# Splitting the row checks, row sums on ScalarE, and a new end for the first stream: an fp32 gated graph network followed by a graph convolution

## The chip, the cores and the metric

One core of one Trainium2 chip. The metric is the device time of the kernel in microseconds (us), the median of three runs. The core's engines are TensorE (PE, with its weight loads PEld), VectorE (DVE), ScalarE (ACT), GpSimd (POOL) and SyncE (SP, which here only issues DMAs).

## The reference

16 graphs of N = 1024 nodes with C = 128 features, fp32. `adj` holds 0 and 1 and is symmetric by its construction. The node mask is all ones.

```python
def _gru_cell(m, h, w_ih, w_hh, b_ih, b_hh):
    ...
    r = sigmoid(xr + hr); z = sigmoid(xz + hz)
    n = tanh(xn + r * hn)
    return (1.0 - z) * n + z * h

def _L0_gnn_ref(x, adj, mask, weight, w_ih, w_hh, b_ih, b_hh):
    h = x
    for i in range(4):
        hw = einsum('bnc,cd->bnd', h, weight[i])
        m = einsum('bjn,bjd->bnd', adj, hw)
        h = _gru_cell(m, h, w_ih[i], w_hh[i], b_ih[i], b_hh[i])
    return h * mask[:, :, None]

def _L1_gnn_ref(x, adj, W, b, gamma, beta):
    h = x
    for i in range(4):
        h = einsum('bnm,bmc->bnc', adj, h @ W[i]) + b[i]
        h = relu(h)
        mu, var = mean(h, axis=(0, 1)), variance(h, axis=(0, 1))
        h = gamma[i] * (h - mu) * rsqrt(var + EPS) + beta[i]
    return h

x = x + _L0_gnn_ref(relu(layernorm(x)), adj, nodemask, ...)
x = x + _L1_gnn_ref(relu(layernorm(x)), adj, ...)
```

## The kernel before

A first phase, here the gate phase, computes the gated layers, a second one, conv, the convolution layers, and a third one writes the output. Features lie on the partitions and nodes along the row (128x1024), cut in two halves of 512 nodes[...].

**The gate phase** has two streams: `sa` takes the graphs 0, 2, ..., 14 and `sb` the graphs 1, 3, ..., 15. `half_step(one, two)` (L1095) lets PE aggregate for stream `one` (32 matmuls `pm <- row, ghw` at L524, adjacency rows against a split of hW into a high and a low fp32r part) while stream `two` passes its gates: 12 fp32 products at L993, each 128x512 and recorded as two matmuls, for r, n and z of both halves. The two change places after each half-step, so a cycle of four layers has eight half-steps, and there are 64 in all. `clock[0]` counts half-steps. Every engine's order in this phase is the order in which the program calls (`manual_schedule`), and work that isn't part of a half-step is put on an agenda: `at(n, place, fn)` enters it for half-step n, and `due(place)` runs it at a named place.

In a half-step, stream `two` does for each half: the products; `reset_gate` (ACT L1011, sigmoid of r); `candidate` (DVE L1012 r*hn, L1013 + xn, then ACT L1016 tanh); `less` (DVE L1029); `update_gate` (ACT L1020, sigmoid of z; DVE L1033); `mixed` (DVE L1034, the new h). ACT's `high` (L919 or L938) and DVE's `low` (L926 or L942) make the split of hW of stream `one`. At its end `agg_rows` copies `pm` to `m` on ACT (L955); the next half-step's products start with `g_r <- h` and go on with `g_r <- m`. The PSUM banks are reused: the second half's `g_hn` needs the bank that L1012 of the first half reads, and the second half's `g_z` the bank that L1020 reads.

**The next graph's rows.** While a stream is in its last layer (i = 3), `fetch` (L853) asks SP for rows 0 to 3 of the adjacency of the graph after next in this stream, into a staging area of four slots; POOL casts them to fp32r (`round_rows`, L577); `last_four` (L866) then checks them, and asks for rows 4 to 7 in the same slots. The check reads the low 16 bits of each value and tells whether the rounding was exact: on ACT it is a `glance` (L586, an activation with a sum, two instructions in the trace), on DVE a `look` (L610, a maximum). For `sa` (its i = 3 half-step is called A here) rows 4 to 7 are looked at by DVE at "start" of the next half-step (B); in B the staging serves `sb`, whose rows 4 to 7 are glanced at on ACT at "gap" of the half-step after (C).

The transposed adjacency goes to DRAM for conv (`adjT_d`, POOL casts at L615, SP transposes, POOL stores, `mids` at L1088). h is not transposed by PE between layers: `half_out` writes a DVE transpose of 32x32 blocks, `exchange_out` and `exchange_in` (or `pair_in`) bring it back by DMA with the blocks in place. Only the last h of the graphs 14 and 15 is turned by PE, in `tail_sums` (L735, `pt_x`), since `last_tail` (L757) calls it without exchanged parts; its inner `rest` normalizes (L668 to L680, `rs_mid`, `ms_mid`, `y_mid`) and stores y for conv.

**Conv.** For each layer and graph b, `load_adjT` brings eight rows of the transposed adjacency in bf16 (`block`, `packed`), and ACT and DVE widen them to fp32r (L1311, L1313), into the same slots that the rows of the gate phase use. `aggregate` does 32 matmuls of L524. In layer 0 PE takes the adjacency before the weights: `first_split` (L1366) loads y and splits it (chw, ACT L1370, DVE L1371); after b's aggregation, `first_weights` copies it out of PSUM (cm, ACT L1380) and multiplies with the weights (`pw`, L1381), two for each graph; this is called half an aggregation later. Here PE, POOL and SP follow the program's calls around the end of the gate phase, and the remaining order on ACT and DVE is made by the framework's scheduler. `row_sums` (L1402) has PE sum the rows of graph 0's adjacency into all partitions (`pt_deg`, L1407), which ACT copies to `degree` (L1411); `raw_weights` uses it from layer 1 on.

Of the kernel before, what the change touches and what calls it, by code (L numbers as in the profile page):

```python
# [16 lines left out]
P = 128  # L17
# [324 lines left out]
def exact_path(  # L342
# [39 lines left out]
    def tmp(name):  # L382
        return ps_t.tile([P, HALF], F32, tag="tmp", name=name)

    adjT_d = [dram.tile([NB, P, N], BF16, tag=f"adjT{b}", name=f"adjT_d{b}") for b in range(B)]
    xmid_d = [dram.tile([N, C], F32, tag=f"xmid{b}", name=f"xmid_d{b}") for b in range(B)]
    ymid_d = [dram.tile([P, N], F32, tag=f"ymid{b}", name=f"ymid_d{b}") for b in range(B)]
# [20 lines left out]
    nc.vector.memset(eps_t, EPS)  # L408
    ones = const.tile([P, 1], F32, tag="ones", name="ones")
    nc.vector.memset(ones, 1.0)  # L410
    low = const.tile([P, (B + 2) * NB], F32, tag="low", name="low")
    nc.vector.memset(low, 0.0)

# [119 lines left out]
    with ExitStack() as st:  # L533
# [51 lines left out]
                k = b * NB + j  # L585
                nc.scalar.activation(junk, lows, AF.Copy, accum_out=low[:, k : k + 1])  # L586

        def exchange_out(t, name, d=None):
            if d is None:
                d = rawd.tile([P, HALF], F32, tag="cross", name=f"cross_{name}", bufs=8)  # L590
            nc.sync.dma_start(d, t)
            return d

        def exchange_in(d, t):
# [2 lines left out]
            for s in range(4):  # L597
                nc.sync.dma_start(t[s * 32 : (s + 1) * 32, :].rearrange("r (t x) -> r t x", t=4), src[s])

        def pair_in(d, t):  # L600

            src = d.rearrange("h (t r) (s x) -> s r (h t) x", t=4, s=4)
            for s in range(4):
                nc.sync.dma_start(t[s * 32 : (s + 1) * 32, :].rearrange("r (a x) -> r a x", a=8), src[s])

        def look(b, row, j, part=0):

# [108 lines left out]
                half_out(cross_tile(f"t_{name}_{hf}"), src, hf, name, d[hf])  # L716
            return d

        def half_out(t, src, hf, name, d=None):
            turned = nc.vector.transpose(by_nodes(t), four_ways(src[:, hf * HALF : (hf + 1) * HALF]))  # L720
            return exchange_out(t, f"{name}_{hf}", d), turned

        def cross_tile(name):
            return half_tile(name).bitcast(F32)
# [30 lines left out]
            nc.gpsimd.dma_start(ymid_d[b], y)  # L755

        def last_tail(b, xt, hT):  # L757
            nt = tail_sums(b, xt, hT)
            y = y_mid(b) if b + 1 < B else xt.rearrange("p k c -> p (k c)")
            store_xmid(b, xt)  # L760

            def rest():
                norm_apply(xt, y, nt)
                store_ymid(b, y)

            return rest
# [3 lines left out]
        class Stream:  # L770
# [54 lines left out]
            def plan(self, n, tail=None):  # L825

                if tail:
                    b, xt, hT, parts = tail
                    end = {}

                    def sums():
                        end["norm"] = tail_sums(b, xt, hT, parts)

                    def blocks(hf):
                        if hf == 0:
                            end["y"] = y_mid(b)
                        norm_blocks(xt, end["y"], end["norm"], range(hf * BH, (hf + 1) * BH))

                    at(n + 2, "gap", sums)
                    at(n + 3, "mid", lambda: store_xmid(b, xt))  # L840
                    at(n + 3, "gap", lambda: norm_factors(end["norm"]))
                    at(n + 4, "beside0", lambda: blocks(0))
                    at(n + 4, "beside1", lambda: blocks(1))
                    at(n + 5, "mid", lambda: store_ymid(b, end["y"]))
                if self.b + 2 < B:
                    at(n + 5, "mid", self.next_load)
                    at(n + 6, "start", self.next_sums)
                    at(n + 6, "gap", self.next_factors)
                    at(n + 7, "beside0", lambda: self.next_blocks(0))
                    at(n + 7, "beside1", lambda: self.next_blocks(1))  # L850
                    at(n + 7, "end", self.ins_away)

            def fetch(self):  # L853

                if self.i == 3 and self.b + 2 < B and not written[0]:
                    if self is sa:
                        t = turned_tile(f"stage{self.b + 2}").bitcast(F32)
                        room[0] = [t[:, 2 * q : 2 * q + 2, :].rearrange("p a n -> p (a n)") for q in range(4)]
                    self.stage = room[0]
                    stage_rows(self.b + 2, self.stage, range(4))  # L860

            def first_four(self):
                if self.stage:
# [2 lines left out]
            def last_four(self):  # L866
                if self.stage:
                    b, stage, self.stage = self.b + 2, self.stage, None
                    glance(b, stage, range(4))
                    stage_rows(b, stage, range(4, NB))  # L870
                    self.rows += round_rows(b, stage, range(4, NB))

                    def looks():
                        for j in range(4, NB):
                            look(b, stage[j % 4], j)

                    if self is sa:
                        at(clock[0] + 1, "start", looks)
                    else:
                        at(clock[0] + 1, "gap", lambda: glance(b, stage, range(4, NB)))  # L880

            def take(self):
                self.xt, self.y = self.next_x, self.next_y
# [6 lines left out]

            def half_away(self, hf):

                if self.i + 1 - hf == L and self.b + 2 < B:
                    if hf == 0:
                        self.pair = rawd.tile([NH, P, HALF], F32, tag="pair", name=f"pair_out{self.b}", bufs=4)
                    half_out(cross_tile(f"t_out{self.b}_{hf}"), self.new, hf, f"out{self.b}", self.pair[hf])
                elif self.turned_away(self.i + 1 - hf):
                    nm = f"{self.b}_{self.i + 1 - hf}"
                    out, self.last_dve = half_out(cross_tile(f"t_h{nm}_{hf}"), self.new, hf, f"h{nm}")
                    self.outs.append(out)  # L900
# [138 lines left out]
            def finish(self):  # L1039

                if self.i < L:
                    return
                args = self.b, self.xt, self.hT
                self.b, self.i = self.b + 2, 0
                if self.b >= B:
                    self.rest = last_tail(*args)
                    return
                self.take()
                ins, outs, h_in = self.next_ins, self.pair, self.hT
                parts = [args[-1][:, hf * HALF : (hf + 1) * HALF] for hf in range(NH)]  # L1050

                last = args[-1]
                at(clock[0] + 1, "ins", lambda: pair_in(ins, h_in))
                at(clock[0] + 1, "outs", lambda: pair_in(outs, last))
                self.plan(clock[0], (*args, parts))
# [3 lines left out]
        def at(n, place, go):  # L1059
            agenda.setdefault((n, place), []).append(go)  # L1060
# [5 lines left out]
        def first_step(one, two, gated, halfway):  # L1066
# [10 lines left out]
            feed.some(1)  # L1077
            two.gate_step(1)
            two.half_away(1)
            gated()  # L1080
            one.agg_step(0)
            halfway()
# [12 lines left out]
        def half_step(one, two, gated=None, halfway=None):  # L1095
# [18 lines left out]
            two.products(0)  # L1114
            two.reset_gate(0)
            due("beside0")
            two.candidate(0)
            two.less(0)
            one.high(0)
# [9 lines left out]
            two.products(1)  # L1129
            two.reset_gate(1)  # L1130
            due("beside1")
            one.low(1)
            two.candidate(1)
            two.less(1)
# [20 lines left out]
        with tc.manual_schedule(engines=every):  # L1155
# [115 lines left out]

            sa.plan(0)
            sb.plan(1)
            first_step(sa, sb, looks, lambda: ahead(1))
            first_step(sb, sa, lambda: turn_ih(prep, w_g, 2), lambda: ahead(2))
            written[0] = False
# [6 lines left out]
        with tc.manual_schedule(engines={getattr(mybir.EngineType, e) for e in ("PE", "Pool", "SP")}):  # L1283
            sb.gate_step(0)
            sb.gate_step(1)
            with tc.issue_after(sb.last_act.ins):
                sa.rest()
            sb.finish()


    worst = small.tile([P, 1], F32, tag="worst", name="worst")
# [74 lines left out]
    def first_split(b):  # L1366
        yt = flat(f"y{b}").rearrange("p k c -> p (k c)")
        nc.gpsimd.dma_start(yt, ymid_d[b])
        hw = hw_tiles(b, f"chw{b}_0")
        nc.scalar.copy(hw[0], yt)  # L1370
        nc.vector.tensor_sub(hw[1], yt, hw[0].bitcast(F32))  # L1371
        return hw

# [17 lines left out]
    def raw_weights(i, pm, aff, stats):  # L1391
# [6 lines left out]
            nc.vector.scalar_tensor_tensor(mt[:, cols], degree[:, cols], aff[1], mt[:, cols], ALU.mult, ALU.add)  # L1398
            nc.tensor.matmul(pc[hf], w_c[:, i, :], mt[:, cols], start=True, stop=True)
        conv_done(0, i, pc, stats)  # L1400

    def row_sums(rows):  # L1402

        pd = [tmp(f"pt_deg{hf}") for hf in range(NH)]
        for j in range(NB):
            for hf in range(NH):
                nc.tensor.matmul(  # L1407
                    pd[hf], ones_r, rows[j][:, hf * HALF : (hf + 1) * HALF], start=(j == 0), stop=(j == NB - 1)
                )
        for hf in range(NH):  # L1410
            nc.scalar.copy(degree[:, hf * HALF : (hf + 1) * HALF], pd[hf])  # L1411

    xo = []

# [29 lines left out]
            for n0, n in pieces(k):  # L1444
                nc.gpsimd.dma_start(xo_piece(k, n0, n), by_node(xmid_d[k], n0, n))

    ones_r = work.tile([P, P], F32R, tag="ones_r", name="ones_r", bufs=1)
    nc.vector.tensor_copy(ones_r, ones.to_broadcast([P, P]))
    degree = w_mT.rearrange("p l c -> p (l c)")[:, :N]

    stats = small.tile([P, B * NH, 6], F32, tag="bn_st", name="stats0")
# [1 line left out]
    for b in range(B):  # L1453
# [9 lines left out]
        if b == B - 1:  # L1463
            hw_next = raw_split(1)
        aggregate(pm, hw, rows, 1)
        if b == 0:
            row_sums(rows)
        hw, waiting = hw_next, (b, pm)


# [112 lines left out]
```

## Time and profile before

| | us |
|---|---|
| median of three runs | 1788.79 |
| fastest, slowest run | 1787.79, 1789.32 |
| the profiled execution | 1789.26 |
| its span | 1787.5 |
| one half-step of the gate phase | 17.57 |
| aggregation of graph 0 in conv begins at | 1166.99 |
| output phase, from | 1759.3 |

The profile belongs to one execution. Its timeline has one line for a group of neighbouring instructions: start, time from first start to last end, engine, line of the kernel, operation, output <- input, shape, count, and in brackets the idle time before it and what ended that. Ends of PE instructions are modelled, and the first matmul after an fp32 product is recorded some 0.4 us early, so intervals between starts are a better measure on PE than busy time. In the table of waits a line gives who waited, for whom, the sum in us, the number of waits and the longest.

### The profile page before, as it was taken

Reading aid. Unit: us, or ns where it says so; the run is one execution under the profiler, and the core shown is the slowest. Engines: PE = TensorE matmul, PEld = TensorE weight load, DVE = VectorE, ACT = ScalarE, POOL = GpSimd, SP = SyncE. Lnnn points to the kernel's source line nnn. Section 1 sums busy time; section 2 is a strip of 40 time slices with the busy share of each in tenths; the row PEclk is TensorE's granted clock in tenths of the full one; section 3 lists DMA queues with packets and bytes.
Section 4 is the critical chain, followed back from the end, with each engine's and each line's share of the span. In section 5 each row is a group of like instructions: output and inputs, shape, how many; then the busy total and the mean of one; then the engine's idle time right before and its main releaser. Section 6 shows DMA issues by size and latency. Waiting matters only on the chain. (4 is left out here: it accounts for less than half of the span.)

```text
span 1787.5 us, 22335 instructions
## 1 busy us (share of the span) xinstructions
PE 1759.3 (98%) x6734; PEld 1191.7 (67%) x6734; DVE 1305.9 (73%) x2310; ACT 1107.6 (62%) x1713; POOL 379.3 (21%) x417
## 2 busy tenths in 40 slices
PE   9999999999999999999999999999999999999997
PEld 6565655565656565556555556577778888888886
DVE  7677877887887787887797787676666666666665
ACT  5356556556566556665655655476777767768765
POOL 4314323332331331422432333010100000000011
PEclk9999999999999999999999999999999999999999
DMA  7467657777676676776756768788766575767667
GB/s 259 135 175 262 189 163 272 179 208 241 204 200 213 223 212 197 245 202 202 260 169 186 265 174 227 256 287 311 271 228 241 207 253 201 245 224 245 238 217 268
DMA packets 363617, 400.16 MB, mean 224 GB/s; under 512 B 158188, under 2 KB 239888, under 8 KB 363488
## 3 DMA queue, kind: packets, MB, share of 16 engines
q1 hardware_dynamic: 342736, 323.59, 57.6%
q0 software_dynamic: 20224, 74.80, 11.3%
q8 instruction: 55, 0.90, 0.2%
q14 instruction: 74, 0.61, 0.1%
q10 hardware_dynamic: 528, 0.26, 0.0%
HBM read 267.47 MB, written 97.52 MB: 204 GB/s over the span
## 5 line engine op out<-in xcount | busy, mean ns | idle before, releaser
L524 PE MATMUL pm<-row,ghw 128*128 128x512 f32 x2048 | 503.6, 402 | 0.7 <-DVE ghw L926 0.6
L524 PEld LDWEIGHTS pm<-row,ghw 128*128 128x128 f32 x2048 | 383.8, 188 | 106.6 <-issue 29.2
L1016 ACT ACTIVATE r<-r,vecs 128x512 f32<-128x512 f32 x128 | 92.6, 723 | 255.0 <-DVE r L1013 253.1
L524 PE MATMUL pc_m<-wide,chw 128*128 128x512 f32 x1024 | 245.3, 395 | 0.0
L615 POOL CAST half<-row 128x1024 bf16<-128x1024 f32 x128 | 147.4, 1161 | 361.1 <-DMA adjT<-half 347.9
L524 PEld LDWEIGHTS pc_m<-wide,chw 128*128 128x128 f32 x1024 | 190.4, 188 | 41.9 <-issue 3.8
L524 PE MATMUL pc_g_r<-wide,chw 128*128 128x512 f32 x464 | 186.9, 403 | 0.3 <-ACT chw L501 0.3
L524 PE MATMUL pc_g_z<-wide,chw 128*128 128x512 f32 x464 | 181.0, 390 | 0.0
L577 POOL CAST row<-stage 128x1024 fp32r<-128x1024 f32 x112 | 128.6, 1156 | 243.7 <-DMA stage<-in_adj_dram 232.2
L1012 DVE SCALAR_TENSOR_TENSOR r<-g_hn,vecs,r 128x512 f32<-128x512 f32 x128 | 93.3, 729 | 117.9 <-ACT r L1011 66.9
L955 ACT COPY m<-pm 128x512 f32<-128x512 f32 x128 | 68.4, 585 | 163.5 <-PE pm L524 163.5
L1313 DVE CAST wide<-block 128x1024 fp32r<-128x1024 bf16 x160 | 109.9, 692 | 75.5 <-PE pc_m L524 48.3
L1313 DVE CAST wide<-packed 128x1024 fp32r<-128x1024 bf16 x160 | 110.1, 691 | 71.9 <-PE pc_g_z L524 53.5
L1311 ACT CAST wide<-packed 128x1024 fp32r<-128x1024 bf16 x96 | 100.6, 1048 | 58.5 <-PE pc_m L524 29.7
L993 PE MATMUL g_r<-m,w_mT 128*128 128x512 f32 x256 | 132.0, 597 | 3.4 <-ACT m L955 2.9
L1311 ACT CAST wide<-block 128x1024 fp32r<-128x1024 bf16 x96 | 100.7, 1049 | 53.9 <-PE pc_g_z L524 27.7
L993 PE MATMUL g_z<-m,w_mT 128*128 128x512 f32 x256 | 130.7, 592 | 0.0
L993 PE MATMUL g_xn<-m,w_mT 128*128 128x512 f32 x256 | 130.7, 592 | 0.0
L1361 DVE BATCH_NORM_STATS2 stats<-feat 128x6 f32<-128x512 f32 x128 | 84.1, 686 | 47.0 <-ACT feat L1360 45.9
L1029 DVE TENSOR_TENSOR h<-h,r 128x512 f32<-128x512 f32 x96 | 83.8, 872 | 41.9 <-ACT r L1016 41.8
L1033 DVE TENSOR_TENSOR h<-h,z 128x512 f32<-128x512 f32 x128 | 107.8, 842 | 6.8 <-ACT z L1020 0.2
L1011 ACT ACTIVATE r<-g_r,brz 128x512 f32<-128x512 f32 x128 | 87.9, 686 | 39.1 <-PE g_r L993 38.8
(186 smaller groups left out, 2830.5 us busy)
## 6 DMA issues: line engine op xcount, KB each, us to landing
block<-adjT_d SPq DMA_DIRECT2D x256, 256.0 KB, 4.7
packed<-adjT_d SPq DMA_DIRECT2D x256, 256.0 KB, 5.5
stage<-in_adj_dram SPq DMA_DIRECT2D x120, 512.0 KB, 5.7
adjT_d<-adjT POOLq DMA_DIRECT2D x16, 2048.0 KB, 7.7
cross_h<-t_h SPq DMA_DIRECT2D x92, 256.0 KB, 2.2
n_h<-cross_h SPq DMA_DIRECT2D x368, 64.0 KB, 2.0
xmid_d<-x POOLq DMA_DIRECT2D x16, 512.0 KB, 6.9
y<-ymid_d POOLq DMA_DIRECT2D x16, 512.0 KB, 5.4
```

Source lines behind the costliest of these rows:

```text
L524: nc.tensor.matmul(pm[hf], hw[s][:, j * P : (j + 1) * P], rows[j][:, hf * HALF : (hf + 1) * HALF], start=(j == 0 and s == 0), stop=(j == N ...
L577: nc.gpsimd.tensor_copy(t, stage[j % 4])
L615: nc.gpsimd.tensor_copy(t, row.bitcast(F32))
L993: nc.tensor.matmul(po, wT[:, i, g * C : (g + 1) * C], rhs, start=start, stop=stop)
L1011: nc.scalar.activation(r, pr, AF.Sigmoid, bias=brz[:, 3 * i : 3 * i + 1])
L1012: nc.vector.scalar_tensor_tensor(r, phn, b_hn(i), r, ALU.add, ALU.mult)
L1016: nc.scalar.activation(self.r, self.r, AF.Tanh, bias=b_in(self.i))
L1029: nc.vector.tensor_sub(ho, hin, self.r)
L1033: nc.vector.tensor_mul(ho, ho, self.z)
L1311: nc.scalar.copy(r, t)
L1313: nc.vector.tensor_copy(r, t)
L1361: nc.vector.bn_stats(stats[:, b * NH + hf, :], dst)
```

## The change

Five things are changed.

- The checks of a graph's rows are split. `fetch` asks for rows 0 and 1; a new `fetch_more`, after the first half's `reset_gate`, for rows 2 and 3. A new `first_glances`, after the second half's `reset_gate` and ahead of its `candidate`, checks rows 0 and 1, and `last_four` only rows 2 and 3. The looks of `sa`'s rows 4 to 7 come two at "start" and two at a new place "looks", after "beside0" in the first half and ahead of its `candidate`; the glances of `sb`'s come two at "beside1" and two at "gap".
- The load of x of the next graph (`next_load`) moves from "mid" of half-step n + 5 to a new place "late" in the second half of n + 4.
- The row sums of graph 0 are made in the gate phase, by ACT activations with a sum over `sa`'s rows at clocks 5 to 8, one column of `by_row` each; `by_row` is written to DRAM (`degree_d`) at clock 9, and in conv POOL loads it into all partitions of `degree`. PE's `pt_deg`, the two copies and the matrix of ones go.
- The last h of `sa` (graph 14) is exchanged by DMA too, through POOL's queue, so that `tail_sums` has exchanged parts; `sb`'s (graph 15) still is turned by PE.
- `sa`'s end, formerly `last_tail` at the finish of its last half-step and `rest` after `sb`'s last activation, is called whole (`sa.last()()`) after `sb.finish()`, issued after `sb`'s last DVE instruction. The chw copy of `first_split` is issued after `sb`'s last copy of m.

```diff
-        def exchange_out(t, name, d=None):
+        def row_sums(rows, js):
+            for j in js:
+                junk = work.tile([P, N], BF16, tag="junk", name=f"summed{j}", bufs=1)
+                nc.scalar.activation(junk, rows[j].bitcast(F32), AF.Copy, accum_out=by_row[:, j : j + 1])
+
+        def exchange_out(t, name, d=None, eng=nc.sync):
...
         def last_tail(b, xt, hT):
-            nt = tail_sums(b, xt, hT)
+            parts = None
+            if b + 1 < B:
+                parts = [hT[:, hf * HALF : (hf + 1) * HALF] for hf in range(NH)]
+            nt = tail_sums(b, xt, hT, parts)
...
-                    at(n + 5, "mid", self.next_load)
+                    at(n + 4, "late", self.next_load)
...
-                    stage_rows(self.b + 2, self.stage, range(4))
+                    stage_rows(self.b + 2, self.stage, range(2))
+
+            def fetch_more(self):
+                if self.stage:
+                    stage_rows(self.b + 2, self.stage, range(2, 4))
...
-                    glance(b, stage, range(4))
+                    glance(b, stage, range(2, 4))
                     stage_rows(b, stage, range(4, NB))
                     self.rows += round_rows(b, stage, range(4, NB))
-                    def looks():
-                        for j in range(4, NB):
-                            look(b, stage[j % 4], j)
-
                     if self is sa:
-                        at(clock[0] + 1, "start", looks)
+                        for place, js in (("start", (4, 5)), ("looks", (6, 7))):
+                            at(clock[0] + 1, place, lambda js=js: [look(b, stage[j % 4], j) for j in js])
                     else:
-                        at(clock[0] + 1, "gap", lambda: glance(b, stage, range(4, NB)))
+                        for place, js in (("beside1", (4, 5)), ("gap", (6, 7))):
+                            at(clock[0] + 1, place, lambda js=js: glance(b, stage, js))
+
+            def first_glances(self):
+                if self.stage:
+                    glance(self.b + 2, self.stage, range(2))
...
-                if self.i + 1 - hf == L and self.b + 2 < B:
+                if self.i + 1 - hf == L and (self.b + 2 < B or self is sa):
+                    eng = nc.sync if self.b + 2 < B else nc.gpsimd
...
                 if self.b >= B:
-                    self.rest = last_tail(*args)
+                    if self is sa:
+                        pair_in(self.pair, args[-1], nc.gpsimd)
+                        self.last = lambda: last_tail(*args)
+                    else:
+                        self.rest = last_tail(*args)
                     return
...
             two.products(0)
             two.reset_gate(0)
             due("beside0")
+            due("looks")
+            two.fetch_more()
             two.candidate(0)
             two.less(0)
...
             two.products(1)
             two.reset_gate(1)
             due("beside1")
+            two.first_glances()
+            due("late")
             one.low(1)
             two.candidate(1)
...
+            for n, place, js in (
+                (5, "beside1", (0,)),
+                (6, "beside0", (1,)),
+                (6, "beside1", (2,)),
+                (6, "gap", (3,)),
+                (7, "gap", (4, 5, 6)),
+                (8, "start", (7,)),
+            ):
+                at(n, place, lambda js=js: row_sums(sa.rows, js))
+            at(9, "mid", lambda: nc.gpsimd.dma_start(degree_d.rearrange("(j p) -> p j", p=P), by_row))
...
             sb.gate_step(1)
-            with tc.issue_after(sb.last_act.ins):
-                sa.rest()
             sb.finish()
+            with tc.issue_after(sb.last_dve.ins):
+                sa.last()()
...
         hw = hw_tiles(b, f"chw{b}_0")
-        nc.scalar.copy(hw[0], yt)
+        with tc.issue_after(sb.last_m.ins):
+            nc.scalar.copy(hw[0], yt)
...
         aggregate(pm, hw, rows, 1)
-        if b == 0:
-            row_sums(rows)
+        if b == 2:
+            nc.gpsimd.dma_start(degree, degree_d.partition_broadcast(P))
```

## The prediction, made before the changed kernel ran

> **What bounds the kernel now.** I read the page's busy shares and clock first, then the table of waits, then the timeline of TensorE with those of the engines it waits for.
>
> ```profile
> PE 1759.3 (98%) x6734; PEld 1191.7 (67%) x6734; DVE 1305.9 (73%) x2310; ACT 1107.6 (62%) x1713; POOL 379.3 (21%) x417
> ...
> PEclk9999999999999999999999999999999999999999
> ```
>
> TensorE (PE) is busy 98% of the span at full clock, so time leaves only where PE stands still or has less to do. Its records overlap, so I measure by starts: at full pace an aggregation matmul starts 0.227 us after the one before, a gate product (two records) takes 0.86 us, a half-step (32 matmuls, 12 products) 17.57 us. Whatever a start is late beyond that is a stall. The table of waits names the releasers, but gives only the idle time that the overlap leaves visible:
>
> ```profile
> PE g_z L993 <- ACT z L1020: 5.0, 8, 0.7
> PE g_hn L993 <- DVE r L1012: 4.6, 6, 1.2
> ```
>
> One cycle (eight half-steps, 143 us) shows how much hides behind these. PE's timeline, start and length first:
>
> ```profile
> 299.37 1.02 PE L993 MATMUL g_r<-m,w_mT 128*128 128x512 f32 x2
> 301.54 1.13 PE L993 MATMUL g_hn<-h,w_hhT 128*128 128x512 f32 x2 [1.15 <-DVE r L1012]
> 302.50 1.02 PE L993 MATMUL g_xn<-m,w_mT 128*128 128x512 f32 x2
> 304.18 1.12 PE L993 MATMUL g_z<-h,w_hhT 128*128 128x512 f32 x2 [0.66 <-ACT z L1020]
> 305.14 1.02 PE L993 MATMUL g_z<-m,w_mT 128*128 128x512 f32 x2
> ...
> 313.30 1.02 PE L993 MATMUL g_r<-h_in,w_hhT 128*128 128x512 f32 x2
> 314.38 1.12 PE L993 MATMUL g_r<-m,w_mT 128*128 128x512 f32 x2
> ```
>
> The steps 299.37 to 301.54 and 302.50 to 304.18 are 1.31 and 0.82 us too long, and the product after each pause runs 0.1 longer: 1.42 and 0.92. Step 313.30 to 314.38 loses 0.22 + 0.1 = 0.32 in the same way. What runs ahead of the releasers, on VectorE (DVE) and ScalarE (ACT):
>
> ```profile
> 293.62 1.22 DVE L610 TENSOR_REDUCE low<-stage 128x1 f32<-128x1024 uint16 x1 [1.08 <-DMA stage<-in_adj_dram]
> 295.33 1.22 DVE L610 TENSOR_REDUCE low<-stage 128x1 f32<-128x1024 uint16 x1 [0.49 <-DMA stage<-in_adj_dram]
> 298.24 2.59 DVE L610 TENSOR_REDUCE low<-stage 128x1 f32<-128x1024 uint16 x2 [1.69 <-DMA stage<-in_adj_dram]
> 300.74 0.74 DVE L1012 SCALAR_TENSOR_TENSOR r<-g_hn,vecs,r 128x512 f32<-128x512 f32 x1
> ```
> ```profile
> 312.70 1.06 ACT L586 ACTIVATE junk<-stage 128x1024 bf16<-128x1024 uint16 x1
> 313.67 0.19 ACT L586 ACTIVATION_READ_ACCUMULATOR junk<-stage 128x1 f32 x1
> 313.76 1.05 ACT L955 COPY m<-pm 128x512 f32<-128x512 f32 x2
> ```
>
> Four looks and their waits for rows hold DVE until 300.8, so L1012 is late and its bank comes free late; four glances end at 313.9, so the copies of m start late. The same subtraction over all starts of the gate phase gives three sums: g_hn behind DVE 6.25 us (six places), g_z behind ACT 6.31 (seven), g_r behind m 6.68 (thirteen, the largest 1.26 at 905.7; one, 0.61 at 1138.6, is due to a copy of chw). One stall of 0.84 stands at 651.5, at L524, behind a slow ghw subtraction (3.05 us). Together 20.1 us. From 1148 to 1745 I find nothing comparable.
>
> **What the Trainium skill says.** "Perfetto Trace Analysis", section "Tensor Engine Instruction (MATMUL, LD_WEIGHTS)", closing note: ACT and DVE run strictly in order, and a TensorE end time is an estimate. The trace agrees: m stands behind glances whose results it doesn't need, and PE's records overlap. "SBUF — State Buffer", section "SBUF: two separate sides": DVE and GpSimd (POOL) share a port pair that one instruction holds to its end. The trace has 0.69 us for a DVE subtraction alone and 1.3 to 1.5 beside POOL casts. "TensorE: Matmul & The Clock Gate", Part 1: after about 3.4 us idle the array runs at half rate, and warms in about as long. Here transposes of the start (pt_idle) begin 213 ns apart, later ones 109; no pause of that length occurs in between.
>
> **The change part by part.** All sums are against the profiled execution, 1789.26 us (span 1787.5 and 1.8 around it), 0.47 over the median 1788.79.
>
> *Looks and glances.* A look costs 1.22 us on DVE, a glance 1.06 + 0.19 on ACT; none is saved, all are split two and two. Half-step A (275.8 to 293.4): two glances go ahead of the second tanh, where ACT idled 2.50 us to 287.63; the last two then end near 291.3, before m at 293.4. B: only two looks precede L1012, which I put at 297.9 for the first half; the other two stand behind it, ahead of `less(0)`. Working forward by the durations above, z of half 0 is done at 300.6, and g_z of half 1 needs it at 301.95; g_hn needs its bank at 300.2. Both stalls go with 1.3 to 2.3 us to spare. Two of sb's glances, whose rows I expect at 301 to 302, end at 303.9, before the tanh of half 1 (304.9). C: two glances use ACT's 4.49 us idle ahead of 325.87. So the m copies in B and C are on time. The loads of rows 2 and 3 are issued after the reset of the gate instead of before; on SP's queue, which issues them, nothing else changes place in this phase. As the glances that free a stage slot end earlier, rows 4 to 7 are asked for 3 to 5 us earlier. All of the 20.07 but the 0.84 should go: **-19.2**. If rows land late, ACT waits in front of a tanh: from nothing to more than the 19.2 (third rival).
>
> *The x load* moves one half-step earlier, with its POOL issue (0.89 us). DVE waited 15.8 us in 14 for x, beside PE's work. Cost 0; if issue and casts hold the port pair, up to 0.8 in a cycle, 5 in all.
>
> *Row sums.* PE loses 16 matmuls, 1178.30 to 1182.05: **-3.75**. Two ACT copies go. Eight activations of about 1.25 us (glance price, f32 input) come in, clocks 5 to 8, in idle ACT time: three in one gap run 128.96 to 132.7 before m at 133.35. The one at clock 8's start puts off the first r by about 1.2 us, where PE has no use of it yet for longer. The write of 1,024 separate 4-byte elements and the 512 KB broadcast on POOL's queue are asynchronous, needed a layer later: 0, at most 0.5.
>
> *First stream's last h exchanged.* Eight pt_x transposes go, 1155.47 to 1156.34: **-0.87**. Two DVE transposes (0.7 us each) and six POOL DMAs come in; the data is wanted some 7 us after conv starts, and I expect landing at its start: 0.
>
> *sa's end behind sb's, and chw after last_m.* The chw copy leaves the m at 1138.6 (counted above); two of them, 2.1 us, now stand before sb's last sigmoid: 3.0 instead of 1.9 us after the gates begin, while g_hn's bank is needed at 6.9 and has it at 5.1. But the end of sa queues on ACT ahead of what PE needs. Before:
>
> ```profile
> 1170.38 3.19 ACT L680 ACTIVATE y_mid<-x,ms_mid,rs_mid 128x128 f32<-128x128 f32 x8 [0.94 <-DVE ms_mid L676]
> ...
> 1177.23 1.06 ACT L1380 COPY cm<-pc_m 128x512 f32<-128x512 f32 x2
> ```
> ```profile
> 1182.73 1.02 PE L1381 MATMUL pw_g_hn<-cm,w_c 128*128 128x512 f32 x2
> ```
>
> Let T0 be the start of conv's first aggregation, 1166.99 before. In the new program order ACT has, after sb's last z: a wide cast; chw of b=2, which needs the buffer of the aggregation that ends at T0+8.3 (to 9.5); the table load 1.28; rs_mid, which waits for sa's statistics, now behind sb's tail on DVE (12.3); two casts (14.4); eight y_mid blocks, after ms_mid at 15.5 (18.7); two casts (20.75); chw (21.8); a cast (22.85); then the two copies cm, the first done at T0+23.5. PE is through both aggregations at T0+15.6 and takes pw in order: **+7.9**, between 5 and 11 as the DVE tail shifts; 0 only if ACT catches up earlier than its order permits. Such a pause exceeds the skill's 3.4 us; half rate for one window costs 0 to 1.7 (estimate, that page): **+0.8**. Later cm copies have slack (b=2 ready T0+36, needed 37.6).
>
> Sum: -19.2 - 3.75 - 0.87 + 7.9 + 0.8 = -15.1, giving 1774.1 by the profiled time, 1773.7 by the median.
>
> **The rivals.**
> - *No pause at the transition.* For: the earlier trace has no PE pause there. Against: the order of cm. 1773.7 - 8.7 = 1765.
> - *Glances hidden by half.* Rows arrive as late as now and L1012 waits behind the second pair of looks: 9.6 of the 19.2 stay, 1783. For: rows landed one by one before each look (idle 1.08, 0.49, 1.69). Against: they are requested earlier.
> - *Slower: glances that wait in front of the tanh.* ACT is in order. In A and B the first two glances now stand ahead of the second tanh; behind it come z, two glances and the m copies, which PE waits for. By the schedule above these have 2.1 us to spare (291.3 to 293.4; in B a little more). Rows that land x later than ACT comes to them cost PE x - 2.1 in two half-steps of seven cycles. At x = 3.2 that is 14 x 1.1 = 15.4 and eats the whole gain; at 3.5 it is 19.6, and the time -19.2 - 4.6 + 8.7 + 19.6 = +4.5, 1793. For: DVE's looks waited for landings. Against: those waits were 0.5 to 1.7, and the loads are issued no later.
> - *The change doesn't do what it says*: stalls pass to another wait of the same length (say ghw's subtraction, slow beside POOL). Then only -4.6 + 8.7 remains: 1793, counted with the case before.
>
> **How the numbers follow.** Forecast 0.55, no pause 0.17, half hidden 0.18, the slower two together 0.10. Forecast: **1773.7**. The range reaches to 1763.5 (no pause, a little less of rest) and 1783.5 (half hidden); it leaves the slower cases and tails out. About 0.2% (3.6 us) is the smallest difference a measurement of this kernel tells from none. Half hidden with an 11 us pause, and part of the slower cases, fall within it: 0.05. Faster 0.88, slower 0.07.
>
> **What would show it.** Right: the waits g_hn behind DVE r and g_z behind ACT z vanish from the table, g_r behind m falls below 1 us in all; no pt_deg; eight pt_x transposes fewer; and between b=1's aggregation and pw one pause of 5 to 11 us whose releaser is ACT cm. Wrong: pauses at A, B or C behind tanh or ghw, with ACT idle "<-DMA stage" ahead of L586; a pause elsewhere in the transition, or none.

## The result, and the profile after

The changed kernel takes 1815.19 us (median of four runs, 1813.81 to 1817.45) where the kernel before takes 1788.8. The ratio is 1.0147, with a 95% interval of 1.0131 to 1.0163: slower by 26 us. Forecast were 1773.7 us, and a range from 1763.5 to 1783.5: the forecast is missed by 41.5 us. The profiled execution took 1817.45, its span is 1815.6.

The page of the changed kernel, busy shares, then the table of waits for PE alone (who waited for whom, sum in us, times, longest):

```profile
PE 1764.6 (97%) x6710; PEld 1196.5 (66%) x6710; DVE 1276.6 (70%) x2311; ACT 1115.3 (61%) x1727; POOL 374.1 (21%) x424
```
```profile
PE g_z L1011 <- ACT z L1038: 25.9, 9, 4.6
PE pw_g_hn L1419 <- ACT cm L1418: 6.8, 1, 6.8
```

The waits of g_r for m are gone and g_hn for r is down to 0.4 us, as forecast, and so is `pt_deg`; the pause before pw is there, as forecast. New is a wait for z of up to 4.6 us, once in each cycle, and in another half-step than A, B or C. PE's timeline at one of them, then ACT's:

```profile
376.98 1.02 PE L1011 MATMUL g_xn<-m,w_mT 128*128 128x512 f32 x2
382.58 1.43 PE L1011 MATMUL g_z<-h,w_hhT 128*128 128x512 f32 x2 [4.58 <-ACT z L1038]
383.80 1.92 PE L1011 MATMUL g_z<-m,w_mT 128*128 128x512 f32 x2
```
```profile
373.91 0.72 ACT L1034 ACTIVATE r<-r,vecs 128x512 f32<-128x512 f32 x1
381.33 0.62 ACT L937 CAST ghw<-n_h 128x512 fp32r<-128x512 f32 x1 [6.70 <-DMA n_h<-cross_h]
381.85 0.68 ACT L1038 ACTIVATE z<-g_z,brz 128x512 f32<-128x512 f32 x1
```

PE waits for the bank that z of the first half reads, z stands on ACT behind the cast of hW of the other stream, and that cast waits 6.70 us for `n_h`, the h that comes back by DMA. PE then runs at half rate for a while (the next product is recorded with 1.92 instead of 1.02). So the chain is PE, ACT, a transfer. What lay in the queues then (DMA issues from 362 to 384 in the changed kernel, with KB each and the median from issue to landing):

```profile
adjT_d<-adjT POOLq DMA_DIRECT2D x1, 2048.0 KB, 8.1
cross_h<-t_h SPq DMA_DIRECT2D x2, 256.0 KB, 5.6
xmid_d<-x POOLq DMA_DIRECT2D x1, 512.0 KB, 10.4
x<-in_x_dram POOLq DMA_DIRECT2D x1, 512.0 KB, 13.2
n_h<-cross_h SPq DMA_DIRECT2D x8, 64.0 KB, 6.2
```

In the same half-step of the kernel before (359 to 378) there is no load of x, and the exchange is quicker:

```profile
cross_h<-t_h SPq DMA_DIRECT2D x3, 256.0 KB, 2.9
...
n_h<-cross_h SPq DMA_DIRECT2D x8, 64.0 KB, 2.0
```

That points to the x load, which the change has moved into this half-step. It was the first theory, and only half of the truth.

The starts of PE tell how much is where. Below, "gate excess" is the sum, over the half-steps, of the interval between the starts of two aggregations less 17.57; 10 to 14 us of it belong to the first five half-steps, which include the set-up. "Conv" is from the first aggregation of conv to the first output transpose. Both are from the profiled execution, medians from all timed runs; e9's profiled execution was its slowest, 3.8 us over its median. One slow execution of e16, of 9599.64 us, is left out of its median.

| kernel | median us | gate excess | conv |
|---|---|---|---|
| before | 1788.8 | 31.0 | 591.5 |
| changed | 1815.2 | 49.3 | 597.4 |
| e1 x back | 1791.8 | 26.1 | 598.1 |
| e5 glances alone | 1770.6 | 13.6 | 591.5 |
| e9 changed, aligned | 1781.0 | 20.4 | 596.2 |
| e10 glances + 32 bytes | 1785.5 | 27.4 | 591.5 |
| e13 aligned, x back | 1777.7 | 12.2 | 596.7 |
| e14 the same, sa's end later | 1768.1 | 10.4 | 587.8 |
| e16 before + 32 bytes | 1796.2 | 42.3 | 591.5 |

### The profile page after: what moved, and what is told of

The parts are those of the page before. It is cut to its first block, busy times and chain, and to the rows that moved or that the text cites. A ratio compares the mean times of both kernels' runs of the same rounds, so it can differ in the third digit from the quotient of the medians.

```text
span 1815.6 us, 22286 instructions
## 1 busy us (share of the span) xinstructions
PE 1764.6 (97%) x6710; PEld 1196.5 (66%) x6710; DVE 1276.6 (70%) x2311; ACT 1115.3 (61%) x1727; POOL 374.1 (21%) x424
## 5 line engine op out<-in xcount | busy, mean ns | idle before, releaser
L526 PE MATMUL pm<-row,ghw 128*128 128x512 f32 x2048 | 510.5, 406 | 1.5 <-DVE ghw L944 1.4
L526 PEld LDWEIGHTS pm<-row,ghw 128*128 128x128 f32 x2048 | 387.9, 190 | 111.7 <-issue 32.1
L623 POOL CAST half<-row 128x1024 bf16<-128x1024 f32 x128 | 141.6, 1118 | 412.7 <-DMA adjT<-half 397.7
L1030 DVE SCALAR_TENSOR_TENSOR r<-g_hn,vecs,r 128x512 f32<-128x512 f32 x128 | 93.4, 730 | 159.1 <-ACT r L1029 88.4
L1011 PE MATMUL g_z<-m,w_mT 128*128 128x512 f32 x256 | 135.7, 613 | 0.0
L1011 PE MATMUL g_z<-h,w_hhT 128*128 128x512 f32 x192 | 100.4, 605 | 25.3 <-ACT z L1038 25.3
L1047 DVE TENSOR_TENSOR h<-h,r 128x512 f32<-128x512 f32 x96 | 76.3, 795 | 47.8 <-ACT r L1034 47.6
```

The lines of the kernel that those rows point to most:

```text
L526: nc.tensor.matmul(pm[hf], hw[s][:, j * P : (j + 1) * P], rows[j][:, hf * HALF : (hf + 1) * HALF], start=(j == 0 and s == 0), stop=(j == N ...
L623: nc.gpsimd.tensor_copy(t, row.bitcast(F32))
L1011: nc.tensor.matmul(po, wT[:, i, g * C : (g + 1) * C], rhs, start=start, stop=stop)
L1030: nc.vector.scalar_tensor_tensor(r, phn, b_hn(i), r, ALU.add, ALU.mult)
L1047: nc.vector.tensor_sub(ho, hin, self.r)
```

## The experiments

Each is compared with runs of the kernel before on the same chip; its medians there were 1790.3, 1789.8, 1789.6 and 1791.0 for the four groups e1 to e4, e5 to e8, e9 to e12 and e13 to e16.

### First group: the x load, and the end of the first stream

**e1.** The x load goes back.

```diff
-                    at(n + 4, "late", self.next_load)
+                    at(n + 5, "mid", self.next_load)
```

> The changed kernel with the load of the next x put back to the middle of half-step n + 5. Theory X (the x load, third in a burst behind the stores of adjT_d and xmid, holds up the exchange of h, for which ACT waits in front of z): the wait of L937 for n_h and PE's wait for z go, 39.7 us of late half-steps in the profiled run vanish, time 1774 to 1778. Rival S (the two stores alone do it, since they start 3.95 us into the half-step now and 2.01 before): the stalls stay mostly, over 1800. Rival G (the split glances displace the cast in front of z): same, over 1800. The pause before pw stays at 6.9 us in all theories.

Measured 1791.84, ratio 1.0004 (0.9994 to 1.0014). 23.4 us less than the changed kernel, but 14 above what the theory wanted. Short pauses for z remain, and others (`g_hn` behind DVE's r) stand in the half-step of x's sums, which now wait for x on DVE.

**e2.** The same line, the other way, in the kernel before (with `due("late")` where the changed kernel has it).

> The kernel before with only the load of x moved to the late place of half-step n + 4. Theory X: pauses for z appear in one half-step of each cycle, slower by 15 to 40 us (1804 to 1829), less than in the changed kernel if the stores start 2 us earlier here. Rivals S and G: within 3 us of before, 1786 to 1792.

Measured 1792.35, ratio 1.0005 (0.9993 to 1.0017). The move as such costs the kernel before nothing that shows. So the x load isn't harmful by itself; something in the changed kernel takes the room that it needs.

**e3.** On e1; sa's end in its old place.

```diff
-            sb.finish()
-            with tc.issue_after(sb.last_dve.ins):
+            with tc.issue_after(sb.last_act.ins):
                 sa.last()()
+            sb.finish()
```

> The load of x back, and sa's end called after sb's last activation and before sb's finish, with the exchanged h and all else kept. Theory T (the pause before pw is the ACT queue: the end of sa stands in front of cm): cm still stands behind rs_mid and y_mid, but these no longer wait for sb's tail on DVE, so the pause falls from 6.9 to between 1 and 5 us; 2 to 6 us faster than the run with x back alone. Rival (the pause comes from late landings of adjacency rows or of y): within 1 us of that run.

Measured 1795.94, ratio 1.0028 (1.0015 to 1.0041), 4 us slower than e1. The pause before pw fell from 8.3 to 3.3 us (by starts), as expected; but a new one of 5.3 stands before it, at sb's `pt_x` behind DVE's h. DVE's timeline there:

```profile
1169.76 1.14 DVE L749 SCALAR_TENSOR_TENSOR x<-h,maskT,x 128x128 f32<-128x128 f32 x4 [4.90 <-DMA h<-pair_out]
1170.82 0.68 DVE L1047 TENSOR_TENSOR h<-h,r 128x512 f32<-128x512 f32 x1
```

sa's end waits 4.90 us for the exchanged h, in front of sb's last h. The pause was moved, and the exchanged h is what sets the earliest place of sa's end.

**e4.** On e1; only the statistics of sa stay at the end of the gate phase, the normalization (in place in x) comes after graph 0's first weights, and sb's after graph 1's.

```diff
             with tc.issue_after(sb.last_dve.ins):
-                sa.last()()
+                sa.rest = sa.last()
...
-            y = y_mid(b) if b + 1 < B else xt.rearrange("p k c -> p (k c)")
+            y = xt.rearrange("p k c -> p (k c)")
...
-            if b == 1:
+            if b in (1, 2):
                 with tc.issue_after(last.ins):
-                    sb.rest()
+                    (sa if b == 1 else sb).rest()
```

> The load of x back, sa's last statistics after sb's last DVE instruction, but its normalization after graph 0's first weights, and sb's one graph later, both in place in x. Theory T: cm is then ahead of both on ACT, the pause before pw falls under 1 us, 7 to 9.5 us faster than the run with x back alone, 1765 to 1769. Rival (late landings): within 1 us of that run.

Measured 1783.18, ratio 0.9953 (0.9928 to 0.9977): 8.7 below e1, and conv took 587.7 instead of 598.1. So the pause before pw comes from sa's end standing ahead of cm on ACT. The edit also takes away the buffer `y_mid`, for whose store cm waits in the last 0.85 us (shown further below); that share and the order on ACT weren't tested apart. The level is too high, as in e1.

### Second group: where the rest comes from

After e1 to e4 the theory was P: PE's pauses had given the other engines time, and without them something else is always late.

**e5.** The kernel before with the split of looks and glances alone (the parts `fetch`, `fetch_more`, `first_glances`, `last_four` and "looks" of the change's diff).

> The kernel before with only the looks and glances split (fetch_more, first_glances, the new places). As predicted at first: all of 19.2 us of stalls go and nothing comes, about 1770. Theory P (PE's pauses in B gave the other engines time; without them the exchange of h and the arrival of x, both with little to spare, become the late ones): g_hn behind DVE r and g_r behind m go in B and C, but pauses for z at the half-step with the stores and for r at the half-step with x's sums stand instead, some 13 to 17 us together; 1782 to 1788.

Measured 1770.61, ratio 0.9888 (0.9869 to 0.9907). Theory P falls, and the first working of the forecast holds: 19.2 us below its group's kernel before, by the interval 16.6 to 23.4. That it fits to the tenth is luck: by starts, 17.3 of the 20.1 us of stalls are gone, and 2.7 remain. Past the first five, 55 of the 58 half-step intervals are 17.57 to 17.60. PE without a pause in B and C is no problem for the exchange, so what spoils e1 is in the rest: row sums, exchange of the last h, or something that comes with them.

**e6.** The changed kernel, with one of the three transfers that stand in a burst ahead of the exchange (adjT_d, xmid, x) later.

```diff
-                    at(n + 3, "mid", lambda: store_xmid(b, xt))
+                    at(n + 4, "mid", lambda: store_xmid(b, xt))
```

> The changed kernel with the store of xmid (512 KB) one half-step later, so that the x load follows adjT_d directly: the burst ahead of the exchange has two transfers, as in the kernel before, instead of three. Theory B (what counts is how much lies in the queues ahead of cross_h): its landing falls from +15.7 to about +13 into the half-step, the pauses for z from 5 to under 1.5 us a cycle, 1786 to 1792. Rival (the read of x as such is harmful, or its place on POOL): stays over 1805.

Measured 1793.37, ratio 1.0014 (1.0001 to 1.0026). That is 1.4 above the range. In the half-step of the store `cross_h` now lands 10.8 to 13.4 us after its start, and only one of seven has a pause for z, of 0.8 us; half-steps up to 3 us longer come right after it, where xmid went. A burst of fewer bytes does less harm.

**e7.** The changed kernel, with `counts = (3, 2, 1)` for `(2, 2, 1)`.

> The changed kernel with one more transpose of an adjacency row in the half-step after sb's first (counts 3, 2, 1 for 2, 2, 1), so that the store of adjT_d can be issued 1.5 to 3 us earlier ahead of the exchange. Theory B (collision in time): adjT_d starts at about +1 to +2 instead of +3.6 to +3.9, cross_h lands 2 us earlier, the pauses for z fall by a third to a half: 1797 to 1806. Rival (place in time doesn't matter): 1813 to 1818.

Measured 1797.53, ratio 1.0044 (1.0026 to 1.0062), 17.7 below the changed kernel. Where adjT_d was issued 0.2 us into the half-step, it took 0.4 us more than 17.57; where it came at 2.9, 5.2. The collision in time is real.

**e8.** e6's edit, e4's end, x early.

> The changed kernel with xmid stored one half-step later and sa's normalization after graph 0's first weights (x still early). If both theories hold, the burst and the pause before pw are gone and x is there in time for its sums: 1770 to 1779, faster than both kernels. If x's early load still costs by itself: over 1785.

Measured 1785.22, ratio 0.9968 (0.9951 to 0.9985): above the range that was expected if both theories held, and 0.2 over the mark for a cost of the early x by itself. But e4, with x back, is at 1783.2, 2 us less and within the noise, and both lie above 1770 to 1779. So the burst is how the loss comes about, and not the whole of why there is one.

Setting the eight traces side by side showed what the theories had missed: in all kernels with the row sums the DMA transposes, and the exchange with them, were slower, and not only at the pauses: between 40 and 72 us the transposes took 3.2 us in the median, where the kernel before, e2 and e5 have 2.7. In the changed kernel, over the whole run:

```profile
cross_h<-t_h SPq DMA_DIRECT2D x92, 256.0 KB, 2.4
n_h<-cross_h SPq DMA_DIRECT2D x368, 64.0 KB, 2.2
...
adjT<-half SPq DMA_TRANSPOSE x128, 3.3
```

The kernel before, e2 and e5 have 2.2, 2.0 and 2.8 for the three. The change adds a constant tile, `by_row`, 8 fp32 per partition, 32 bytes, ahead of nearly all other buffers. In the built programs (the traces hold no addresses) `half`, `adjT`, `t_h`, `n_h`, `row`, `stage` and the gate phase's `h` begin at multiples of 256 bytes within the partition before, and 32 bytes beyond one after.

### Third group: 32 bytes

**e9.** The changed kernel with that tile widened. All engines keep their instructions in the same order; only addresses differ.

```diff
-    by_row = const.tile([P, NB], F32, tag="by_row", name="by_row")
+    by_row = const.tile([P, 64], F32, tag="by_row", name="by_row")[:, :NB]
```

> The changed kernel with by_row in a tile of 256 bytes per partition instead of 32 (its first 8 columns are used), nothing else: each engine's instructions keep their order, but the SBUF addresses of all buffers that come after it (adjT, half, t_h, n_h, row, stage, h, x) are multiples of 256 again, as in the kernel before; the changed kernel has them at 32 beyond. Theory A (alignment: transfers to and from SBUF that start off a 256-byte boundary take longer, which removes the slack of the exchange): the DMA transposes fall from 3.3 to 2.8 us and cross_h from 2.4 to 2.2, the pauses for z go, and the time is 1771 to 1777, what was forecast at first. Rival D (the 4 KB tile degree_d in DRAM shifts the DRAM buffers, or ACT's row sums upset the order of things): stays over 1800.

Measured 1780.96, ratio 0.9947 (0.9930 to 0.9963): 34.2 us less than the changed kernel, from one line. Its DMAs over the whole run:

```profile
cross_h<-t_h SPq DMA_DIRECT2D x92, 256.0 KB, 2.2
n_h<-cross_h SPq DMA_DIRECT2D x368, 64.0 KB, 2.0
...
adjT<-half SPq DMA_TRANSPOSE x128, 2.8
```

degree_d is still there, so its place in DRAM isn't the cause. 4 us above the expected range remained.

**e10.** e5's kernel with a tile that nothing uses.

```diff
+    pad = const.tile([P, 8], F32, tag="pad", name="pad")
+    nc.vector.memset(pad, 0.0)
     low = const.tile([P, (B + 2) * NB], F32, tag="low", name="low")
```

> The kernel with only the split looks and glances (1770.6 us), with an unused tile of 32 bytes per partition ahead of the other buffers. Theory A: the DMA transposes take 3.3 us again, pauses come in the half-steps with the stores and with x's sums, 1782 to 1792. Rival D: 1769 to 1772.

Measured 1785.49, ratio 0.9975 (0.9967 to 0.9983): 14.9 above e5. The first 1140 us of e5 and of e10, from the view by windows (busy us of PE, PEld, DVE, ACT and POOL with counts, then PE's clock, the share of the DMA engines, GB/s):

```profile
0.00:1140.00 1140.00, 1134.10 (x3668) 685.05 (x3669) 875.61 (x1638) 666.18 (x1152) 345.62 (x369) 1.00 0.70 215
```
```profile
0.00:1140.00 1140.00, 1125.35 (x3614) 673.09 (x3615) 866.34 (x1614) 656.58 (x1141) 342.95 (x369) 1.00 0.75 211
```

The DMA engines are busier (0.75 against 0.70) and move less. That is the mark of the shift. The engines' own instructions keep their lengths: among those that come more than 20 times on DVE, ACT and POOL, no kind has a median that differs by more than 0.02 us between e5 and e10. And the pauses are of the same two kinds as in e1, in e10's table of waits:

```profile
PE g_z L1001 <- ACT z L1028: 6.9, 10, 1.3
PE g_hn L1001 <- DVE r L1020: 2.7, 4, 1.1
```

**e11.** The same with a pad of 64 bytes.

> The same with an unused tile of 64 bytes. Theory A with any start off 256 bytes alike: as with 32 bytes. If 64 bytes are enough of an alignment: 1769 to 1772, and transposes of 2.8 us. Rival D: 1769 to 1772 as well, with the same times of the DMAs for both pads.

Measured 1784.0, ratio 0.9970 (0.9957 to 0.9982), transposes 3.3. As with 32.

**e12.** e9 with e4's end.

> The changed kernel with by_row in 256 bytes and sa's normalization after graph 0's first weights. Theories A and T (ACT queue ahead of cm) together: no pause left in gate phase or transition, 7 to 9.5 us below e9: 1763 to 1768. If alignment isn't it: over 1800.

Measured 1775.19, ratio 0.9911 (0.9893 to 0.9929): 5.8 below e9, less than the 7 to 9.5 expected, and above the range. Conv took 587.7, 8.5 less than in e9, so the end did its work; the gate phase has pauses for z as in e9.

### Fourth group: what is left

**e13.** e9 with the x load back (e1's edit).

> The changed kernel with by_row in 256 bytes and the load of x back in the middle of half-step n + 5. If the early load is what still holds up the exchange when the addresses are aligned: the pauses for z (5 to 8 us over the run) go, 1772 to 1776. If it is harmless then: 1779 to 1783. The pause before pw stays near 6.7 us.

Measured 1777.74, ratio 0.9927 (0.9910 to 0.9943). The gate excess falls from 20.4 to 12.2: in e9 the early x still made pauses. By medians the early load costs 3.2 us when aligned, and 23.4 when not. The time is 1.7 above the range: what is left is the transition. PE's waits:

```profile
PE pw_g_hn L1419 <- ACT cm L1418: 6.5, 1, 6.5
...
PE g_z L1011 <- ACT z L1038: 1.6, 2, 1.0
```

**e14.** e13 with e4's end.

> The same with sa's normalization after graph 0's first weights: 7 to 9.5 us below e13, 1763 to 1768, faster than every kernel here.

Measured 1768.09 (1768.0 to 1768.39), ratio 0.9873 (0.9857 to 0.9890): 0.1 above the range and the fastest of all. Against the changed kernel it is 47 us. Its gate excess past the first five half-steps is 0.3.

**e15.** e5 with a pad of 128 bytes.

> The kernel with the split looks and glances only, with an unused tile of 128 bytes. If only starts at multiples of 256 are short: transposes of 3.3 us, 1780 to 1790 as with 32 and 64. If 128 is enough: 2.8 us and 1769 to 1772.

Measured 1782.78, ratio 0.9956 (0.9941 to 0.9971), transposes 3.3. So 128 isn't enough; of the offsets tried (0, 32, 64, 128) only a multiple of 256 is short.

**e16.** The kernel before with the pad of 32 bytes.

> The kernel before with an unused tile of 32 bytes. If the shift only takes slack away: transposes of 3.3 us, but its own pauses leave time for part of it, 1789 to 1797. If it costs by itself wherever it is: 15 us or more, over 1803.

Measured 1796.2, ratio 1.0031 (1.0020 to 1.0042), transposes 3.3. The same shift costs 5 us here, 15 in e5's kernel, 14 in e13's (e1 against it), and 34 with the early x. The DMA transposes are slowed alike, and conv, whose loads land in shifted buffers too, takes 591.5 us in e5, e10 and e16; what the shift costs depends on how much room PE has behind the transfers.

## Why the prediction was wrong

*Looks and glances, -19.2: right in kind and, within the noise, in size* (e5). In the changed kernel's B, DVE has L1030 first and the two looks behind it:

```profile
301.77 0.75 DVE L1030 SCALAR_TENSOR_TENSOR r<-g_hn,vecs,r 128x512 f32<-128x512 f32 x1 [1.79 <-PE g_hn L1011]
302.62 0.69 DVE L1031 TENSOR_TENSOR r<-g_xn,r 128x512 f32<-128x512 f32 x1
303.23 2.33 DVE L618 TENSOR_REDUCE low<-stage 128x1 f32<-128x1024 uint16 x2
```

L1030 waits for PE now and not PE for it. The third rival's wait exists, and costs nothing: ahead of the second tanh in B

```profile
310.21 1.06 ACT L588 ACTIVATE junk<-stage 128x1024 bf16<-128x1024 uint16 x1 [3.53 <-DMA stage<-in_adj_dram]
...
316.46 1.07 ACT L973 COPY m<-pm 128x512 f32<-128x512 f32 x2 [0.45 <-PE pm L526]
```

ACT waits 3.53 us for the row and still waits 0.45 for PE at m. The rival's sum gives x - 2.1, so 1.4 us lost here; nothing was lost. The glances stand in front of a tanh that wasn't ready either: DVE's L1031, which makes its input, ended only at 309.58 + 0.69 = 310.27.

*Row sums, -3.75 and then "0, at most 0.5": the step that failed.* PE's saving is there: with the pause before pw removed, e4, e12 and e14 have a conv of 587.7 against 591.5. But the cost of bringing the sums there was put at nothing: it listed instructions and transfers, and not the new tile. `by_row` takes 32 bytes per partition ahead of the big buffers and shifts them all; this is worth 34.2 us with the early x (changed against e9, same order of instructions) and 14.1 without it (e1 against e13), where 0 was forecast. The Trainium skill has the rule, in "DMA: Bandwidth & Descriptors", section "How a descriptor splits into AXI transactions": a descriptor that doesn't start at a multiple of 256 bytes also fetches the bytes from the boundary below, which are not used and still cost beats of the bus. The runs agree on the boundary (0 against 32, 64 and 128 bytes). That extra fetches are the mechanism inside, no run here shows. It was there to be read before; an address was never looked at.

*The x load, "cost 0; up to 0.8 in a cycle, 5 in all": wrong, for a reason that wasn't priced.* The working thought of POOL's issue and of the port pair, and not of the DMA queues: 512 KB behind 2.5 MB of stores, just ahead of `cross_h`. Costs were 3.2 us with aligned buffers (within the 5), 23.4 with shifted ones, and none that shows in the kernel before (e2). The two losses don't add: 3.2 and 14.1 (e1 against e13) alone, 37.5 together. It fits that they use up the same room and that PE pays only for what is beyond it; that was not tested by itself. About 11 of the 37.5 are the half rate after the changed kernel's long pauses: six of them are 24.4 us by starts, and their half-steps and the next ones take 35.1 us more than at full pace. Together the two terms are 37.5 of the 41.5 us by which the forecast was missed.

*sa's end behind sb's, +7.9 + 0.8: mechanism right; the pause shorter and its aftermath longer than forecast.* ACT in the transition of the changed kernel, then PE:

```profile
1196.23 1.05 ACT L1408 CAST chw<-y 128x1024 fp32r<-128x1024 f32 x1 [5.73 <-PE pc_m L526]
...
1202.15 3.20 ACT L688 ACTIVATE y_mid<-x,ms_mid,rs_mid 128x128 f32<-128x128 f32 x8 [0.87 <-DVE ms_mid L684]
...
1209.97 1.07 ACT L1418 COPY cm<-pc_m 128x512 f32<-128x512 f32 x2 [0.85 <-DMA ymid_d<-y_mid]
```
```profile
1203.45 0.39 PE L526 MATMUL pc_g_z<-wide,chw 128*128 128x512 f32 x1
1210.61 2.08 PE L1419 MATMUL pw_g_hn<-cm,w_c 128*128 128x512 f32 x2 [6.77 <-ACT cm L1418]
1212.48 1.92 PE L1419 MATMUL pw_g_xn<-cm,w_c 128*128 128x512 f32 x2
```

T0 is 1188.09; the first pw starts at T0 + 22.5, where 23.5 was forecast, and the last wait of cm is for the store of ymid out of the buffer that it reuses. The pause is 6.9 us by starts, not 7.9. The half rate after it costs more than the 0.8, and more than the 1.7 that the forecast gave as the most: the starts after the pause lose 2.4 us, and conv is 9.6 longer than in e14, which leaves 2.7 beside the pause. Conv grew by 5.9, where -3.75 + 7.9 + 0.8 = 4.95 was forecast. With cm ahead of it in e14:

```profile
1157.26 1.06 ACT L1408 CAST chw<-y 128x1024 fp32r<-128x1024 f32 x1 [5.69 <-PE pc_m L526]
1158.22 1.06 ACT L1418 COPY cm<-pc_m 128x512 f32<-128x512 f32 x2
```

*The rivals.* "Stalls pass to another wait of the same length" came near in number (1793; e1 has 1791.8), but its reason was not the true one, as e5 showed. Without the shift and with x where it was, e13's profiled time is 1777.64, 3.5 above the forecast's 1774.1 for the profiled time. About 2.6 of that lie in the gate phase, most of it at its end: from the last aggregation to conv it takes 20.5 us, where it was 19.2 before and 18.4 was forecast without sa's transposes, with PE waiting for DVE; the remaining 0.9 is spread over the start, conv and the end.

What stays open is which DMAs of the exchange suffer from the shift by themselves and which by standing behind others; single buffers weren't shifted. The fastest transfers give a hint: a transpose takes at least 2.70 us in e5 and 3.06 in e10, so it is longer by itself, but a `cross_h` at least 1.97 and 2.00.

## What to carry to other kernels

A new small tile is part of a change's price: look at the addresses of the buffers that DMAs use, before and after, and round small constants up so that the large ones behind them keep a start at a multiple of 256 bytes. If transfers are slower all through the program, and not only where the order changed, suspect the layout. And when a removed pause is the aim, list what else lives on that room: transfers that were hidden have less of it afterwards, and two costs that share it can be more together than one by one (3.2 and 14.1 us here, and 37.5 together).

## What the runs showed of the hardware that was not expected

- A shift of 32, 64 or 128 bytes in SBUF lengthens a DMA transpose of 128x1024 bf16 from 2.8 to 3.3 us, and the 64 KB pieces of the exchange from 2.0 to between 2.1 and 2.3. The transpose goes from SBUF to SBUF, so DRAM has no part in it.
- A 256 KB store on SP's queue, issued 1.1 to 2.9 us after three transfers of 3 MB in all on POOL's queue, landed 8.8 us after its issue (changed kernel, at 368.4), where 2.4 is the median of the run. In the kernel before, a store issued 0.2 us after adjT_d landed in 2.0 us, and one issued 5.9 us after it in 3.8.
- After the pause of 6.8 us before pw, the matmuls of a product start 0.85 us apart instead of 0.43: half rate. e14, without the pause, has none of this. The 3.4 us of idle time that the prediction took as the limit isn't one in these runs: between 60 us and the output phase all pauses of 3.1 us and more are followed by half rate, and of six between 2.0 and 2.6 us three are (2.0 in e12, 2.4 in e7, 2.5 in the changed kernel) and three are not (2.2 and 2.3 in e6, 2.4 in e11).
